# The key stage of a two-layer kernel rebuilt: tiles in pairs, places broadcast by DMA, four columns of entries summed at once, the weight table spread by two engines

## The chip, the cores and the metric

The kernel is one program on 1 core of a Trainium2 chip. The metric is device time in microseconds (us) for one execution. The kernel before takes 923.84 us in the median of 3 runs (919.55, 923.84, 924.43).

## The reference, cut to what matters

Two transformer-like layers run one after the other on x, which has 8 batches of 256 tokens of 512 numbers. Each layer is a "cond" part, then a feed-forward part, and is added to x. Only the first layer's preparation matters here.

- Cond part of layer 0: attention with a paged cache of keys and values. q, k and v are products of x; q and k are normalised and rotated; the new k and v are written into the cache; each query sees at most 256 keys that end at itself.
- Feed-forward part of layer 0: a gate picks 2 of 8 experts. Each expert's weight matrix is a common 512x512 matrix W plus a sparse correction. There are 4096 sparse entries with places `mask_idx` (row times 512 plus column) that all experts share. Places may repeat, and entries with the same place add up:

```python
deltas = softmax(expert_atom_weights, axis=-1) @ atoms        # (8, 64) @ (64, 4096)
weighted = deltas * sigmoid(importance)                       # (8, 4096)
rows = mask_idx // H
cols = mask_idx % H
vals = einsum('tk,tks->ts', rw, weighted[top_idx])
contrib = segment_sum((xt[:, cols] * vals).T, rows, num_segments=H)
out = xt @ W.T + contrib.T
```

## The kernel before, in words

Everything is float32. The engines are TensorE (PE; its weight loads are shown as PEld), VectorE (DVE), ScalarE (ACT), GpSimd (POOL) and SyncE (SP). SP only starts DMAs; ACT and POOL start some too. Each engine takes its instructions strictly in order. The order on each engine comes from a planner that replays the program with estimated times, except where the code pins it: `tc.keep_in_program_order`, `in_a_row` (L118: several products pinned behind each other), and the whole attention loop, whose PE order is written by hand (L1806).

The kernel's first stage, the stage of keys (L851 to L1578), makes everything that attention needs:

- **Keys and values.** `keys_values(i)` (L1367), for 16 tiles of 128 tokens: four 128x512 products into a PSUM bank `pkv` (three banks), an ACT copy into `kvt` (four buffers), the rotation on DVE (`rotated`, L1284), squares on ACT and their sum on DVE, a square root on ACT, four ACT multiplications, and one 256 KB store to `kv_new` in HBM.
- **The weight table.** `delta_d` in HBM holds, for each of the 512x512 places, 8 numbers, one for each expert (8 MB). It starts as W repeated 8 times: `load_base` (L1395) loads a 128x128 piece of W; `spread_base` (L1400) makes a 128x1024 tile `spread` of it with one ACT copy and stores it (512 KB). There are 16 such pieces and two `spread` buffers. Pieces are loaded in rounds 0 to 7 of the tile loop and spread in rounds 1 to 8.
- **The sparse entries.** 64 small products `pw` (L1438) turn the atoms into values in columns of 128 entries, 32 columns in all. `sum_same(k)` (L1490) treats one column: a PE transpose `prow` puts the 128 places of the column into every row, a DVE comparison gives `same` (which entries share a place), a DVE operation with `below` marks the entries that stood there before (`again`), a product `psm` sums the entries of a place for 8 experts, and ACT copies the result into `sums`. Three columns are done in each round from round 3. `find_places` (L1515) then sends every repeat to a spare row, so that each place is added once. Much later, during attention, POOL adds the sums into `delta_d` (`add_delta`, L1342).
- **Where the old keys lie.** DVE and POOL find blocks of the cache: four masks `near` (L1123 to L1131) are POOL's only long arithmetic in this stage; four small gathers `held_i` (L1099) read the block table. `find_rows(b)` (L1216) makes row lists; `gather_old(b)` (L1252) and `gather_new(b)` (L1261) are four POOL-issued gathers each, from the cache and from `kv_new`.
- **The end.** The queries of batches 0 and 1 are made, the gate's weights are folded through the output weights (`seen_through`, L130), `gather_new(0)` reads `kv_new`, and the loop of attention begins: the first score product is L1656, which needs `KT` (L1630), the turned keys of batch 0. DVE prepares the masks of attention from `posb` (L1634), whose memory was memory of the key stage.

SP's loads and stores stand in one queue in order: a store that waits for its tile holds back all that stand behind it. Each tile buffer that is stored can be written again only when its store has landed.

Of the kernel before, what the change touches and what calls it, by code (L numbers as in the profile page):

```python
# [19 lines left out]
P = 128  # L20
# [71 lines left out]
def two_layer_kernel(ctx: ExitStack, tc: tile.TileContext, io: dict, out: bass.AP):  # L92
# [759 lines left out]
    with ExitStack() as att:  # L852
# [28 lines left out]
        nc.scalar.dma_start(eaw[:, 0, :], io["eaw"])  # L881
        nc.sync.dma_start(blocks[0], xsrc[:, :, :512])

# [3 lines left out]
        nc.sync.dma_start(inv, io["inv_freq"].partition_broadcast(P))  # L887
        gains = {}
        for src in ("k_scale", "q_scale"):
            gains[src] = dp.tile([P, HD], F32, name=f"gain_{src}")  # L890
            nc.sync.dma_start(gains[src], io[src].partition_broadcast(P))
        for k in range(KC):
            nc.scalar.dma_start(wkv[:, k, :], wsrc[:, k, 512:])
        nc.sync.dma_start(blocks[1], xsrc[:, :, 512:1024])
        imp = dp.tile([P, NSC, E], F32, name="imp")
        nc.scalar.dma_start(
            imp.rearrange("p (q k) e -> p q (k e)", q=4),
            io["impT"].rearrange("(q p k) e -> p q (k e)", q=4, p=P),
        )
        mcol_i = dp.tile([P, NSC], I32, name="mcol_i")  # L900
        nc.scalar.dma_start(
            mcol_i.rearrange("p (q k) -> p q k", q=4),
            io["mask_idx"].rearrange("(q p k) -> p q k", q=4, p=P),
        )

        atoms = []
        for j in range(2):
            atoms.append(dp.tile([P, P, NSQ], F32, name=f"atoms{j}", tag="spread", bufs=2))
            for h in range(2):
                q = 2 * h + j  # L910
                nc.sync.dma_start(
                    atoms[j][h * ATOMS : (h + 1) * ATOMS],
                    io["atoms"][:, q * NS // 4 : (q + 1) * NS // 4].rearrange(
                        "a (p k) -> a p k", p=P
                    ),
                )
        for j in range(2, NTB + 1):
            cols = slice(j % NTB * 512, (j % NTB + 1) * 512)
            nc.sync.dma_start(blocks[j], xsrc[:, :, cols])
# [8 lines left out]
        nc.vector.reciprocal(esm, esm)  # L928
        nc.vector.tensor_scalar(share, share, esm, None, ALU.mult)
        nc.vector.tensor_copy(eaw[:, 1, :], share)  # L930

# [7 lines left out]
        for src in ("k_scale", "q_scale"):  # L939
            nc.vector.tensor_scalar(gains[src], gains[src], 1.0, None, ALU.add)  # L940
# [22 lines left out]
        for c in (C1, C2, C3):  # L963
            nc.vector.scalar_tensor_tensor(
                ang, turn, -c, ang, ALU.mult, ALU.add
            )

# [13 lines left out]
        nc.vector.tensor_scalar(nsin, sin, -1.0, None, ALU.mult)  # L981

        def with_gains(ctab, stab, src):
            g1 = gains[src][:, None, lo_].to_broadcast(trig)
            g2 = gains[src][:, None, hi_].to_broadcast(trig)
            nc.vector.tensor_tensor(ctab[:, :, lo_], cos, g1, ALU.mult)
            nc.vector.tensor_tensor(ctab[:, :, hi_], cos, g2, ALU.mult)
            nc.vector.tensor_tensor(stab[:, :, lo_], nsin, g2, ALU.mult)
            nc.vector.tensor_tensor(stab[:, :, hi_], sin, g1, ALU.mult)
# [143 lines left out]
        def find_blocks(psum, rs):  # L1133
# [51 lines left out]
        jf = ap.tile([P, B, NCAND], F32, name="jf")  # L1185
        nc.vector.tensor_copy(jf, j_i)
        nc.vector.tensor_tensor(
            jf, jf, slot0[:, :, None].to_broadcast([P, B, NCAND]), ALU.add
        )
        tbase = ap.tile([P, B, NCAND], F32, name="tbase")  # L1190
        nc.vector.scalar_tensor_tensor(
            tbase,
            jf,
            float(BLOCK),
            kvf[:, :, None].to_broadcast([P, B, NCAND]),
            ALU.mult,
            ALU.subtract,
        )
        nc.vector.tensor_scalar(
            jf, jf, float(NBLK - 1), SKIP, ALU.is_gt, ALU.mult  # L1200
        )
        nc.vector.tensor_tensor(tbase, tbase, jf, ALU.add)
# [5 lines left out]
        nc.vector.tensor_copy(code0, code_i)  # L1208
        nc.vector.tensor_tensor(code0, code0, tbase, ALU.add)
# [6 lines left out]
        def find_rows(b):  # L1216
# [5 lines left out]
            if b > 2:  # L1222
                tc.keep_in_program_order(first)
# [52 lines left out]
        def squares(src, heads, pool):  # L1276

            sq = pool.tile([P, heads, HD], F32, name="sq")
# [5 lines left out]
        def rotated(i, heads, src, ctab, stab, dst, pool):  # L1284
# [3 lines left out]
            xb = pool.tile(full, F32, name="xrot")  # L1288
# [12 lines left out]
        def query_parts(i, xcols, psum, tag, pool, early=False):  # L1301
# [10 lines left out]
            rotated(i, H, q3, qcos, qsin, qr, pool)  # L1312
            ms = squares(q3, H, pool)
# [47 lines left out]
        with proj:  # L1361
            qp = proj.enter_context(tc.tile_pool(name="qp", bufs=3))
            psq = proj.enter_context(tc.tile_pool(name="psq", bufs=3, space=PSUM))
            dw = proj.enter_context(tc.tile_pool(name="dw", bufs=3))
            psd = proj.enter_context(tc.tile_pool(name="psd", bufs=3, space=PSUM))

            def keys_values(i):  # L1367
# [3 lines left out]
                for k in range(KC):  # L1371
                    nc.tensor.matmul(  # L1372
# [6 lines left out]
                kvt = qp.tile([P, 2 * G * HD], F32, name="kvt", bufs=4)  # L1379
                nc.scalar.copy(kvt, pkv)  # L1380
                k3 = kvt[:, : G * HD].rearrange("p (h d) -> p h d", d=HD)
                kr = qp.tile([P, G, HD], F32, name="kr")
                rotated(i, G, k3, kcos, ksin, kr, qp)
                rs = squares(k3, G, qp)
                nc.scalar.activation(rs, rs, AF.Sqrt, bias=epss[:, 0:1], scale=1.0 / HD)
                nc.vector.reciprocal(rs, rs)
                for h in range(G):
                    nc.scalar.mul(k3[:, h, :], kr[:, h, :], rs[:, h : h + 1])
                nc.scalar.dma_start(kv_new[i * P : (i + 1) * P, :], kvt)
                return rs  # L1390

            QD = D // 4
            w0s = {}

            def load_base(c, part):  # L1395
                cols = slice(part * QD, (part + 1) * QD)
                w0s[c, part] = dw.tile([P, QD], F32, name="w0", bufs=4)
                nc.sync.dma_start(w0s[c, part], io["w0T"][c * P : (c + 1) * P, cols])

            def spread_base(c, part):  # L1400

                cols = slice(part * QD, (part + 1) * QD)
                w0 = w0s.pop((c, part))
                spread = dp.tile([P, QD, E], F32, name="spread", bufs=2)
                nc.scalar.copy(spread, w0[:, :, None].to_broadcast([P, QD, E]))
                wdst = delta_d[: D * D, :].rearrange("(c p r) e -> c p r e", p=P, r=D)
                nc.sync.dma_start(wdst[c][:, cols, :], spread)

            def base_weights(i):
                if i < 2 * KC:  # L1410
                    for part in (0, 1):
                        load_base(i // 2, i % 2 * 2 + part)
                if 1 <= i < 1 + 2 * KC:
                    for part in (0, 1):
                        spread_base((i - 1) // 2, (i - 1) % 2 * 2 + part)

            LEAD = 3
            for i in range(LEAD):
                keys_values(i)
                base_weights(i)  # L1420
                if i == 0:
                    pe = psd.tile([P, E], F32, name="pe", tag="psd")
                    nc.tensor.transpose(pe, eaw.rearrange("e h a -> e (h a)"), ident[:E, :E])
                    eawT = dp.tile([P, E], F32, name="eawT")
                    nc.scalar.copy(eawT, pe)
# [4 lines left out]
            pw = [  # L1430
                psd.tile([P, 2, NSQ, E], F32, name=f"pw{h}", tag=f"pw{h}", bufs=1)
                for h in range(2)
            ]
            for j in range(2):
                for k in range(NSQ):
                    for h in range(2):
                        rows = slice(h * ATOMS, (h + 1) * ATOMS)
                        nc.tensor.matmul(  # L1438
                            pw[h][:, j, k, :],
                            atoms[j][rows, :, k],  # L1440
                            eawT[rows, :],
                            start=True,
                            stop=True,
                        )
            nc.scalar.activation(imp, imp, AF.Sigmoid)
            weighted = dp.tile([P, NSC, E], F32, name="weighted")
            for h in range(2):
                span = slice(h * NSC // 2, (h + 1) * NSC // 2)
                nc.vector.tensor_tensor(
                    weighted[:, span, :],  # L1450
                    pw[h].rearrange("p j k e -> p (j k) e"),
                    imp[:, span, :],
                    ALU.mult,
                )


# [28 lines left out]
                pattern=[[-1, P]],  # L1485
                channel_multiplier=1,
# [3 lines left out]
            def sum_same(k):  # L1490
                prow = psd.tile([P, P], F32, name="prow", tag="psd")
                nc.tensor.transpose(
                    prow, mcol[:, k : k + 1].to_broadcast([P, P]), ident
                )
                same = dw.tile([P, P], F32, name="same")
                nc.vector.tensor_scalar(
                    same, prow, mcol[:, k : k + 1], None, ALU.is_equal
                )

                before = dw.tile([P, P], F32, name="before")  # L1500
                nc.vector.tensor_tensor_reduce(
                    out=before,
                    in0=same,
                    in1=below,
                    scale=1.0,
                    scalar=0.0,
                    op0=ALU.mult,
                    op1=ALU.max,
                    accum_out=again[:, k : k + 1],
                )  # L1510
                psm = psd.tile([P, E], F32, name="psm", tag="psd")
                nc.tensor.matmul(psm, same, weighted[:, k, :], start=True, stop=True)
# [993 lines left out]
```

## Time and profile before

| what | us |
|---|---|
| median of 3 runs (lowest, highest) | 923.84 (919.55, 924.43) |
| the profiled execution, own time | 923.56 |
| its span in the profile | 921.8 |
| so around the span | 1.8 |
| first key product starts | 8.28 |
| last of the four masks `near` ends | 43.68 |
| last store to `kv_new` issued | 100.61 |
| first gather from `kv_new` issued | 105.42 |
| first score product (end of the stage) | 117.57 |
| busy in 0 to 117.6: DVE, ACT, POOL | 87.3, 68.3, 45.3 |
| mean granted TensorE clock over the span | 0.989 |

How to read it: all times below count from the start of the span, and a time of the span plus 1.8 us is a time of the execution. The stage of keys is the first 117.6 us. From there to the end the program of the two versions is the same. "Landing" is the time from the start of a DMA's issue to its completion, when whoever waits for it may go on.

### The profile page before, as it was taken

To read this page: it belongs to the slowest core of one execution; us is meant where nothing else is said; L and a number is where in the kernel's file an instruction comes from. 1 tells how busy PE (TensorE), PEld (TensorE's weight loads), DVE (VectorE), ACT (ScalarE), POOL (GpSimd) and SP (SyncE) were. 2 spreads that over 40 slices of the span, in tenths; PEclk is the share of its full clock that TensorE was granted. 3 is DMA by queue.
4 is the path that set the end of the run, shared out by engine and by line. 5 is a ranking of instruction groups with operands and counts; after the bars stand their busy time and mean duration, and the time that the engine had idled before them with its cause. 6 is when DMAs were issued, how large, how long until landed. Compare 5 with 4: busy or idle time off the path is not lost. (4 is left out here: it accounts for less than half of the span.)

```text
span 921.8 us, 14079 instructions
## 1 busy us (share of the span) xinstructions
PE 877.9 (95%) x4740; PEld 478.5 (52%) x4740; DVE 469.4 (51%) x1510; ACT 362.2 (39%) x1005; POOL 368.1 (40%) x354
## 2 busy tenths in 40 slices
PE   6998989999999899989999999999999999999995
PEld 2654445555555455545443334546677776334773
DVE  4887879779778767684111112482022222455321
ACT  3676666665665556542222213411211111444110
POOL 3811355666667200062856752000333333344422
PEclk9899999999999999999999999999999999999998
DMA  7588494414522223084799966992544443333332
GB/s 204 197 315 295 142 300 135 127 23 107 149 69 57 78 77 99 19 293 103 170 290 340 208 112 160 394 333 109 186 101 72 72 75 69 58 59 58 71 39 42
DMA packets 73870, 133.82 MB, mean 145 GB/s; under 512 B 17262, under 2 KB 22894, under 8 KB 73665
## 3 DMA queue, kind: packets, MB, share of 16 engines
q0 software_dynamic: 25008, 43.42, 24.5%
q1 hardware_dynamic: 38208, 74.05, 23.0%
q10 hardware_dynamic: 10576, 15.39, 4.7%
q8 instruction: 40, 0.66, 0.3%
q14 instruction: 38, 0.30, 0.1%
HBM read 89.69 MB, written 51.78 MB: 153 GB/s over the span
## 5 line engine op out<-in xcount | busy, mean ns | idle before, releaser
L2381 DVE TENSOR_TENSOR y<-py,b 32x512 f32<-32x512 f32 (+1 forms) x60 | 41.3, 689 | 168.4 <-PE py L721 122.3
L2365 ACT ACTIVATE hs<-pu,b 128x32 f32<-128x32 f32 (+1 forms) x240 | 54.1, 349 | 169.9 <-PE pu L2339 138.9
L1688 ACT ACTIVATE s<-s,mx,roots 128x384 f32<-128x384 f32 x128 | 89.8, 703 | 53.1 <-DVE mx L1686 52.1
L707 POOL DMA_INDIRECT xs<-g_d,from_i_l x33 | 34.2, 1037 | 173.8 <-issue 87.9
L750 DVE COPY xsT<-pa 128x512 f32<-128x512 f32 x59 | 40.5, 687 | 101.5 <-PE pa L744 101.2
L2339 PE MATMUL pu<-xsT,w 128*128 128x128 f32 x768 | 89.8, 275 | 0.4 <-issue 0.4
L2339 PEld LDWEIGHTS pu<-xsT,w 128*128 128x128 f32 x768 | 87.7, 192 | 1.1 <-ACT g L2252 0.6
L721 PE MATMUL py<-w,hs 128*128 128x512 f32 x192 | 86.3, 593 | 0.0
L1372 PE MATMUL pkv<-wkv,xb 128*128 128x512 f32 x128 | 67.2, 651 | 8.3 <-DMA wkv<-wqkvT 8.3
L767 POOL DMA_INDIRECT out<-y,token_i_l x33 | 50.9, 1544 | 58.0 <-DVE y L2383 31.2
L1673 DVE CUSTOM_DVE_ANT_0 s<-ps,mask 128x384 f32<-128x384 f32 x128 | 67.4, 549 | 6.3 <-PE ps L1656 6.3
L1344 POOL DMA_INDIRECT delta_d<-entries,put_i x32 | 50.9, 1590 | 45.5 <-DMA delta_d<-entries,put_i 36.2
L731 PE MATMUL py<-delta,xsT 128*64 128x512 f32 (+1 forms) x288 | 65.5, 598 | 0.0
L1723 PE MATMUL po<-pT,kv 128*64 128x256 f32 x384 | 57.4, 388 | 7.9 <-ACT pT L1713 4.9
L1711 PEld LDWEIGHTS pp<-ident,s 128*128 128x128 f32 x384 | 42.1, 141 | 37.0 <-issue 23.9
L1305 PE MATMUL pq<-wq,xb 128*128 128x512 f32 x128 | 60.3, 595 | 0.7 <-DVE lg L1753 0.7
L836 PE MATMUL ph<-woT,oT 128*128 128x512 f32 x128 | 60.8, 609 | 0.0
L721 PE MATMUL py<-delta,xsT 128*128 128x512 f32 x128 | 58.5, 596 | 0.0
L2244 PE MATMUL pc<-wc,x1T 128*128 128x512 f32 x128 | 58.5, 596 | 0.0
L1711 PE MATMUL pp<-ident,s 128*128 128x128 f32 x384 | 56.3, 280 | 2.3 <-DVE pT L1713 1.3
L767 POOL DMA_INDIRECT sums_d<-y,token_i_l x26 | 41.2, 1583 | 32.6 <-DMA sums_d<-y,token_i_l 11.8
L1656 PE MATMUL ps<-KT,QT 64*128 64x384 f32 x256 | 53.7, 520 | 0.4 <-DVE KT L1630 0.4
(436 smaller groups left out, 1467.8 us busy)
## 6 DMA issues: line engine op xcount, KB each, us to landing
delta_d<-spread SPq DMA_DIRECT2D x16, 512.0 KB, 5.4
raw<-delta_d SPq DMA_DIRECT2D x16, 512.0 KB, 4.4
w<-fc_w SPq DMA_DIRECT2D x8, 1024.0 KB, 16.2
part<-sums_d SPq DMA_DIRECT2D x32, 256.0 KB, 4.9
w<-fc_w SPq DMA_DIRECT2D x8, 768.0 KB, 10.6
xb<-xT SPq DMA_DIRECT2D x5, 1024.0 KB, 6.0
sums_d<-zero SPq DMA_DIRECT2D x18, 256.0 KB, 5.7
kv_new<-kvt ACTq DMA_DIRECT2D x16, 256.0 KB, 3.5
```

The source lines that it names most:

```text
L721: nc.tensor.matmul(py, xT[:, k, :], of_expert(experts[0])(weights(k)), start=(k == 0), stop=(k == KC - 1),)
L731: lambda k=k, h=h: nc.tensor.matmul(py[h * n : (h + 1) * n, :], xT[:, k, h * n : (h + 1) * n], of_expert(experts[h])(weights(k)), start=(k ...
L767: nc.gpsimd.indirect_dma_start(out=sum_d, out_offset=bass.IndirectOffsetOnAxis(ap=token, axis=0), in_=y, in_offset=None, bounds_check=sum_ ...
L836: nc.tensor.matmul(ph, oTs[i // 2][:, k, (i % 2) * P : (i % 2 + 1) * P], woT[:, k, :], start=(k == 0), stop=(k == KC - 1),)
L1305: nc.tensor.matmul(pq, xcols[:, k, :], wq[:, k, :], start=(k == 0), stop=(k == KC - 1))
L1372: nc.tensor.matmul(pkv, xb[:, k, cols], wkv[:, k, :], start=(k == 0), stop=(k == KC - 1),)
L1673: nc.vector.tensor_tensor_reduce(out=s, in0=ps[:, r, :WU], in1=mask[:, t, :], scale=1.0, scalar=NEG, op0=ALU.add, op1=ALU.max, accum_out=m ...
L1688: nc.scalar.activation(ss[r], ss[r], AF.Exp, bias=mx[:, r : r + 1], scale=root[:, r : r + 1], accum_out=sm[:, r : r + 1],)
L1711: nc.tensor.transpose(pp[:, c, :], part, ident)
L1723: nc.tensor.matmul(po[r * HD : (r + 1) * HD].rearrange("p m q -> p (m q)"), kvs[t + c][:, v0 + r * HD : v0 + (r + 1) * HD], pT[:, 3 * r + ...
L2244: nc.tensor.matmul(pc, x1T[:, k, i * P : (i + 1) * P], wc[:, k, :], start=False, stop=(k == KC - 1),)
L2339: nc.tensor.matmul(pu[:, c, :], w1[:, k, plan.full[s], c * P : (c + 1) * P], xsT[:, k, :], start=(k == 0), stop=(k == KC - 1),)
```

## The change

- **Order of the first loads.** The key weights go first on ACT's queue; the first block of x is loaded in two parts, 128 columns ahead; the second block waits for the first weights. The gains are loaded on ACT's queue and used later; `imp` and `mcol_i` move to SP behind the atoms.
- **Keys in pairs.** Two tiles share one `kvt` (two buffers of a pair); rotation, squares, sum, root and reciprocal are done once for a pair with twice the width; one 512 KB store for a pair. The eight multiplications of a pair remain.
- **The weight table.** The 16 pieces are split in halves of 128x512. The first half of each is spread by POOL (a multiplication by 1.0) into `spread0`, which has one buffer, the second by ACT into `spread1`, which has two; each half is stored by itself (256 KB, 2 KB to a partition), 32 stores in all. Loads are in rounds 5 to 12, spreading in rounds 6 to 13.
- **Values of the entries.** Instead of 64 products with 8 columns each, four products 32x512, one for each group of 32 PSUM partitions, an ACT copy, four transposes and eight DVE products.
- **Sums.** Four columns at a time, in rounds 8 to 15. The places are broadcast to all partitions by four 512 KB DMAs (`spread_places`) and copied by ACT into `prow`; DVE makes `same` and `first` 512 wide; eight products (32x128 and 8x128) go to four groups of partitions of one bank; ACT copies, PE transposes once, ACT copies and DVE takes a minimum.
- **Placement.** `LEAD` is 5 instead of 3 (the entries start after five tiles), `find_candidates` and the query gains move to rounds 6 and 7, several operations are pinned in program order.

```diff
-        nc.scalar.dma_start(eaw[:, 0, :], io["eaw"])
-        nc.sync.dma_start(blocks[0], xsrc[:, :, :512])
+        for k in range(KC):
+            nc.scalar.dma_start(wkv[:, k, :], wsrc[:, k, 512:])
+        nc.sync.dma_start(blocks[0][:, :, :P], xsrc[:, :, :P])
+        nc.sync.dma_start(eaw[:, 0, :], io["eaw"])
...
+        nc.sync.dma_start(blocks[0][:, :, P:], xsrc[:, :, P:512])
...
+        nc.vector.tensor_copy(blocks[1][:, 0, :1], wkv[:, 0, :1])
         nc.sync.dma_start(blocks[1], xsrc[:, :, 512:1024])
...
-                kvt = qp.tile([P, 2 * G * HD], F32, name="kvt", bufs=4)
-                nc.scalar.copy(kvt, pkv)
...
+                t = i % 2
+                if t == 0:
+                    pair.append(qp.tile([P, 2, 2 * G * HD], F32, name="kvt"))
+                kvt = pair[-1]
+                nc.scalar.copy(kvt[:, t, :], pkv)
+                if t == 0:
+                    return None
...
-                nc.scalar.dma_start(kv_new[i * P : (i + 1) * P, :], kvt)
...
+                nc.scalar.dma_start(
+                    kv_new[(i - 1) * P : (i + 1) * P, :].rearrange("(t p) c -> p t c", p=P), kvt
+                )
...
-            QD = D // 4
+            QD = D // 8
...
             def spread_base(c, part):
...
-                spread = dp.tile([P, QD, E], F32, name="spread", bufs=2)
-                nc.scalar.copy(spread, w0[:, :, None].to_broadcast([P, QD, E]))
...
-                nc.sync.dma_start(wdst[c][:, cols, :], spread)
...
+                for h in range(2):
+                    cols = slice((2 * part + h) * QD, (2 * part + h + 1) * QD)
+                    spread = dp.tile([P, QD, E], F32, name=f"spread{h}", bufs=1 + h)
+                    of_all = w0[:, h * QD : (h + 1) * QD, None].to_broadcast([P, QD, E])
+                    if h:
+                        nc.scalar.copy(spread, of_all)
+                    else:
+                        nc.gpsimd.tensor_scalar(spread, of_all, 1.0, None, ALU.mult)
+                    nc.sync.dma_start(wdst[c][:, cols, :], spread)
...
-            LEAD = 3
+            LEAD = 5
...
+            pw = psd.tile([P, 512], F32, name="pw", tag="pw0", bufs=1)
+            in_a_row(
+                (
+                lambda g=g: nc.tensor.matmul(
+                    pw[g * BW : (g + 1) * BW, :].rearrange("c (k p) -> c k p", p=P),
+                    eawT,
+                    atoms[g // 2][:, :, g % 2 * NG : (g % 2 + 1) * NG].rearrange("r p k -> r k p"),
...
-                prow = psd.tile([P, P], F32, name="prow", tag="psd")
-                nc.tensor.transpose(
-                    prow, mcol[:, k : k + 1].to_broadcast([P, P]), ident
-                )
...
+            def spread_places(q):
...
+                nc.sync.dma_start(
+                    rows_i[q], io["mask_idx"][q * n : (q + 1) * n].partition_broadcast(P)
+                )
...
+            def sum_same(k0):
+                ks = slice(k0, k0 + SAME)
+                each = [P, SAME, P]
+                prow = dw.tile(each, F32, name="prow", bufs=2)
...
+                nc.vector.tensor_tensor(
+                    same, prow, mcol[:, ks, None].to_broadcast(each), ALU.is_equal
+                )
...
+                nc.vector.tensor_tensor(
+                    first, same, below[:, None, :].to_broadcast(each), ALU.mult
+                )
+                psm = psd.tile([P, P], F32, name="psm", tag="psd")
...
+                        psm[j * BW : (j + 1) * BW, :],
+                        unit,
+                        first[:, j, :],
...
+                        psm[j * BW : j * BW + E, :],
+                        weighted[:, k0 + j, :],
+                        same[:, j, :],
...
+                nc.tensor.transpose(pst.rearrange("p j c -> p (j c)"), wide, ident)
+                nc.scalar.copy(sums[:, ks, :], pst[:, :, :E])
+                nc.vector.tensor_scalar(again[:, ks], pst[:, :, E], 1.0, None, ALU.min)
...
-                base_weights(i)
...
+                parts = [(c, part) for c in range(KC) for part in range(4)]
+                n0 = 2 * (i - LEAD)
+                for at in parts[n0 : n0 + 2]:
+                    load_base(*at)
+                if i > LEAD:
+                    for at in parts[n0 - 2 : n0]:
+                        spread_base(*at)
...
-                for k in range(summed, min(summed + 3, NSC)):
-                    sum_same(k)
-                    summed = k + 1
+                if i >= 8 and summed < NSC:
+                    sum_same(summed)
+                    summed += SAME
```

## The prediction

> **What bounds the kernel now.** I read, in this order: the page's busy shares, the stretches of the first stage, its groups of instructions, then the timeline of POOL, DVE and PE. The page's chain of waits covers only the last store, so the stage is read from stretches. They show core busy times of PE, PEld, DVE, ACT, POOL, then the clock, the DMA share and GB/s:
>
> ```profile
> 0.00:20.00 20.00, 11.72 (x22) 5.04 (x23) 8.22 (x42) 5.74 (x9) 6.93 (x46) 1.00 0.79 228
> 20.00:30.00 10.00, 10.00 (x69) 8.56 (x68) 9.31 (x38) 5.11 (x8) 7.29 (x6) 0.85 0.23 69
> 30.00:80.00 50.00, 50.00 (x178) 26.31 (x177) 41.04 (x179) 35.60 (x110) 21.18 (x23) 0.96 0.84 296
> 80.00:105.00 25.00, 22.51 (x78) 12.02 (x77) 19.90 (x81) 16.82 (x57) 0.00 (x0) 0.93 0.47 175
> ```
>
> PE has work nearly all the time, DVE 82% of it from 30 to 80; POOL is light. So before, PE with DVE sets the pace of the stage. Its end is in the timeline: gathers of new keys (POOL), the masks' first step (DVE), the first score (PE).
>
> ```profile
> 105.42 1.00 POOL L1267 DMA_INDIRECT kv<-kv_new,idx_new  x1 [29.08 <-DMA kv_new<-kvt]
> 108.04 0.48 DVE L1634 TENSOR_SCALAR posb<-keyf,kvf 128x512 f32<-128x512 f32 x1
> 117.58 0.59 PE L1656 MATMUL ps<-KT,QT 64*128 64x384 f32 x2 [0.42 <-DVE KT L1630]
> ```
>
> From there attention keeps PE busy 176.8 of 182.4 us to 300, so a shift of the first score passes whole to the end. I predict that shift.
>
> **What gets cheaper** (rows of the stage):
>
> ```profile
> L1405 ACT COPY spread<-w 128x1024 f32<-128x1024 f32 x16 | 16.5, 1040 | 6.8 <-DMA delta_d<-spread 3.5 <-PE pw L1438 3.1 <-ACT sums L1513 0.2
> L1496 DVE TENSOR_SCALAR same<-prow,mcol 128x128 f32<-128x128 f32 x32 | 11.2, 349 | 10.4 <-PE prow L1492 9.6
> L1438 PE MATMUL pw<-eawT,atoms 64*128 64x8 f32 x64 | 7.8, 380 | 0.0
> ```
>
> - DVE, sums: removed 32 x (0.349 same + 0.288 before + 0.081 read) = 23.0. Added 8 x (two 512-wide operations at 0.68, the row of the 512-wide sum L1299, + 0.16) = 12.2. DVE, keys: 16 tiles cost 9.1 + 6.8 + 6.6 + 6.6 + 2.7 = 31.8; 8 pairs cost 8 x (2 x 0.41 + 2 x 0.68 + 0.67 + 0.17) = 24.2. Net -18.4.
> - ACT: removed 16.5 (spread) + 6.5 (squares) + 4.8 (roots) + 4.5 (sums) = 32.3; added 16 x 0.59 + 8 x 0.59 + 8 x 0.30 + 8 x (0.59 + 0.28 + 0.2) + 0.6 = 25.7. Net -6.6. The multiplications and the copies of `pkv` stay.
> - PE: `pw` 7.8 becomes 1.5 to 3.1 (L140, four 512-wide records in 1.53) + 0.6 for transposes. The slow clock behind it goes too: 0.85 and 0.81 in 20 to 40 are 3.4 us lost. A column costs 1.14 - 0.86 = 0.28 between two key records, 9.0 in all; eight groups of eight products and a transpose cost 0.6 each if four groups of partitions overlap, 2.0 if not: 4.8 to 16. Net -14 to 0.
> - Start: the first product waited until 8.28 for 256 KB of weights behind 1 MB of x; with 256 KB of x ahead I estimate 5, bounds 3 and 8.3.
> - DMA: +2 MB of broadcast places, 7 us at 296 GB/s, spread over the stage.
>
> By these sums the stage could lose 10 to 14 us. That is a rival, because of the next part.
>
> **What is added on POOL.** In the compiled order POOL does the four `near` masks, the block gathers, then 16 spreads, with the old-cache gathers between them; the first gather from `kv_new` comes after the 15th spread, its other three after the 16th. `spread0` has one buffer, and the instructions wait so: every POOL spread waits until the store of the one before has landed. That is a serial chain of 16 x (compute + hand-over + landing). The end hangs on it twice: on the gathers, and on `posb`, whose memory was the spreads': it waits for the last landing, and DVE's queue of masks, fold and `KT` waits behind it.
>
> ```profile
> L1126 POOL TENSOR_SCALAR near<-far,offp 128x256 f32<-128x256 f32 x4 | 4.4, 1094 | 14.2 <-DVE look L1086 14.1
> L1130 POOL TENSOR_SCALAR near<-near 128x256 f32<-128x256 f32 x4 | 3.7, 920 | 0.2
> L815 POOL COPY delta<-raw 128x1024 f32<-128x1024 f32 x4 | 8.2, 2040 | 5.0 <-DMA raw<-delta_d 5.0
> ```
>
> - *Compute C.* No POOL multiplication of 512 is in the trace. Above: twice L1130, 1.84. Below: half of L815's copy of 1024, 1.02. The row is nearer to the same kind of instruction, with some fixed share: 1.55.
> - *Landing L* of a 256 KB store with 2 KB to a partition is that of `kv_new`; of a 512 KB spread, the second line:
>
> ```profile
> DMA to landing us min/median/max: 2.0/3.5/8.6
> DMA to landing us min/median/max: 2.6/5.4/8.1
> ```
>
>   Bounds 2.0 (quiet) and 8.6. The stage carries 2 MB more than before but stretches; I take 3.2, just under the median. SP's start of the store follows its tile within 0.05 (25.62 + 1.04 to 26.69).
> - *Period* P = 1.55 + 0.05 + 3.2 = 4.8, bounds 3.1 and 10.5.
> - *Start of the chain.* `near` begins when DVE has `far`: 21.6 before. Now DVE must first sum the squares of the first pair: product from 5, first tile 6.2 (as 8.28 to 14.45), second 3.6, copy and squares 1.2, sum 0.7, `far` 0.5: 17.2. `near` and block gathers took 21.71 to 43.68, 22.0. So 39.2; bounds 36 and 43.7.
> - *Gathers inside:* eight at 1.3 (start to start); three in a row take 3.9 against a landing of 3.2, twice: +1.4; row lists that come late: +0.6. Together 2, bounds 0 and 8.
> - *Tail:* from `posb` to the first score 117.57 - 108.04 = 9.5.
>
> Sum: 39.2 + 16 x 4.8 + 2 + 9.5 = 127.5, against 117.57: +9.9. On the profiled execution's own 923.56 that is **933.5**; the median of the runs, 923.84, stands 0.3 above it. The savings of DVE, ACT and PE then lie beside the chain and are worth nothing. ACT's spreads have two buffers, but their stores stand between POOL's in SP's queue, so ACT too is paced by it, and PE behind ACT's `pkv` copies.
>
> Costed at nothing: the moved gains and `imp` (needed later than they land), `find_candidates`, the pins, all covered by the chain; without that cover they are inside the 104 of rival 1. Moving the first weight loads of W from the first rounds behind LEAD costs nothing to the chain, since POOL is not free before 39 anyway.
>
> [...] I stay at the trace's 3.2, since the queues of this stage are not quiet.
>
> [...]
>
> **The rivals.**
> 1. *The stores land quietly and the chain is short* (faster). With C 1.3 and L 2.2 the period is 3.55 and the score would come at 107.5; the other end is PE: 88 of products (55 keys, 13.8 queries, the rest 19) + 5 start + 3 cold clock + about 8 of waits = 104. First score at 104 to 111, so 910 to 917, say **913**. For it: median landings of `kv_new` of 2.0 to 2.3 in 80 to 105. Against it: in 30 to 80 the DMA engines are 84% busy. It decides below a period of 4.2, where 39.2 + 16 P + 11.5 = 117.57.
> 2. [...] Two blocks of x, `wq` and `woT` stand right ahead of POOL's stores on SP; spreads landed in 7.4 to 8.1 in 50 to 60 and 70 to 80. With C 1.8 and L 3.9 the period is 5.75: 39.2 + 92 + 4 + 9.5 = 144.7, **951**.
> 3. *It doesn't matter*: a period of 3.9 to 4.5, within 0.5%, about **924**: the gain of three engines is eaten by the fourth.
>
> **The numbers.** Forecast (periods 4.5 to 5.4) 0.42, rival 2 0.18, rival 3 0.16, rival 1 0.24. Differences within 0.5% (919.2 to 928.5) can't be told from none in this kernel. Faster 0.24, same 0.16, slower 0.60. The range reaches from within rival 1 to rival 2: 911 to 951; forecast and rival 2 alone span 928.5 to 951.
>
> **What would show it.** In the profile after: POOL's spreads with idle time before them released by the DMA `delta_d<-spread`, one period of 4.8 from start to start, the last near 113; DVE, ACT and PE with more idle time than before although their busy sums fall by about 18, 7 and up to 14; `posb` released by that landing; first score near 127. Right in mechanism and wrong in size if only the period differs. Wrong altogether if the spreads follow each other without waiting for a store, if `near` ends before 34, or if the first score waits for PE or for `kv_new` and not for POOL. A half clock after a long PE idle time at the start of attention would add up to 3 us that I have not counted.

## The result and the profile after

| | before | after |
|---|---|---|
| median of 4 runs (lowest, highest), us | 923.60 (919.55, 924.43) | 937.13 (933.57, 941.24) |
| ratio, 95% interval | 1 | 1.0145 [1.0111, 1.0179] |
| the profiled execution: own time, span | 923.56, 921.8 | 941.24, 939.4 |
| first key product starts | 8.28 | 5.08 |
| last `near` ends, first POOL spread starts | 43.68, none | 40.6, 40.60 |
| `posb` starts | 108.04 | 122.88 |
| first score product | 117.57 | 135.29 |

The changed kernel is slower by 13.5 us (forecast: 9.9). The profiled execution of after is the slowest of its four runs, so its own times are read against its span: the first score is 17.7 us later than before, and the span 17.6 us longer. The shift passes whole to the end. The median of before is of one run more than in the table ahead of the prediction. The ratios and intervals, here and below, are those of the record; they differ from the quotients of the medians by up to 0.35% (e5 below: 0.9996, quotient 1.0030), so no smaller difference is read.

The stretches of after; columns as in the table of before (busy PE, PEld, DVE, ACT, POOL, then the clock, the DMA share and GB/s):

```profile
0.00:20.00 20.00, 13.29 (x24) 5.19 (x24) 10.16 (x49) 5.48 (x9) 7.91 (x50) 1.00 0.84 228
20.00:30.00 10.00, 10.00 (x28) 3.73 (x28) 9.93 (x25) 7.25 (x19) 9.67 (x11) 1.00 0.37 123
30.00:80.00 50.00, 41.53 (x147) 19.87 (x145) 29.03 (x85) 27.10 (x71) 29.34 (x23) 0.86 0.71 237
80.00:105.00 25.00, 17.22 (x80) 7.28 (x79) 13.39 (x41) 14.97 (x42) 10.16 (x7) 0.86 0.73 252
```

Between 30 and 105, PE falls from 72.5 us of work to 58.8, DVE from 60.9 to 42.4, ACT from 52.4 to 42.1, and the clock is lower too. Part of the fall is work that is gone (for DVE 16.3 us over the whole stage, as worked out below); the rest is idle time of three engines in a longer stage. POOL's timeline in after says what the stage waits for (start, duration, and in brackets the idle time ahead with what ended it):

```profile
19.17 2.06 POOL L1135 TENSOR_SCALAR near<-far,offp 128x256 f32<-128x256 f32 x2 [11.43 <-DVE far L1129]
...
40.60 1.53 POOL L1453 TENSOR_SCALAR spread<-w 128x512 f32<-128x512 f32 x1
...
50.20 1.66 POOL L1453 TENSOR_SCALAR spread<-w 128x512 f32<-128x512 f32 x1 [4.38 <-DMA delta_d<-spread]
55.02 1.49 POOL L1453 TENSOR_SCALAR spread<-w 128x512 f32<-128x512 f32 x1 [3.17 <-DMA delta_d<-spread]
...
94.13 1.49 POOL L1453 TENSOR_SCALAR spread<-w 128x512 f32<-128x512 f32 x1 [5.90 <-DMA delta_d<-spread]
97.79 1.49 POOL L1453 TENSOR_SCALAR spread<-w 128x512 f32<-128x512 f32 x1 [2.17 <-DMA delta_d<-spread]
102.95 1.49 POOL L1453 TENSOR_SCALAR spread<-w 128x512 f32<-128x512 f32 x1 [3.68 <-DMA delta_d<-spread]
106.70 1.59 POOL L1453 TENSOR_SCALAR spread<-w 128x512 f32<-128x512 f32 x1 [2.26 <-DMA delta_d<-spread]
...
116.92 1.09 POOL L1279 DMA_INDIRECT kv<-kv_new,idx_new  x1 [0.16 <-issue]
118.92 1.49 POOL L1453 TENSOR_SCALAR spread<-w 128x512 f32<-128x512 f32 x1 [0.92 <-issue]
```

This is the chain of the prediction. The profile names the landing of a store ahead of eight of the fifteen spreads that follow the first; ahead of five more it says only "issue", but there too a store landed 0.14 to 0.15 us before the spread began (63.50 ahead of 63.64, for one). The other two, at 69.69 and 81.12, stand right behind gathers. The sixteen take from 40.60 to 120.4, one each 5.22 us ((118.92 - 40.60) / 15). The first gather from `kv_new` stands behind the fifteenth. DVE's timeline shows the other hook:

```profile
122.88 0.49 DVE L1730 TENSOR_SCALAR posb<-keyf,kvf 128x512 f32<-128x512 f32 x1 [3.29 <-DMA delta_d<-spread]
```

`posb` waits for the last landing, as predicted, 14.8 us later than before. Behind it DVE holds back ACT's `wn`, and ACT holds back PE (PE's timeline):

```profile
120.83 1.04 PE L140 MATMUL acc<-wn,gw 128*32 128x512 f32 x2 [2.43 <-ACT wn L139]
...
125.46 3.64 PE L140 MATMUL acc<-wn,gw 128*32 128x512 f32 x6 [3.00 <-ACT wn L139]
...
135.29 1.01 PE L1752 MATMUL ps<-KT,QT 64*128 64x384 f32 x2
```

### The profile page after: what moved, and what is told of

It reads as the page before. It is cut to its first block, busy times and chain, and to the rows that moved or that the text cites. A ratio compares the mean times of both kernels' runs of the same rounds, so it can differ in the third digit from the quotient of the medians.

```text
span 939.4 us, 13996 instructions
## 1 busy us (share of the span) xinstructions
PE 879.9 (94%) x4728; PEld 469.5 (50%) x4728; DVE 465.1 (50%) x1397; ACT 361.6 (38%) x984; POOL 397.5 (42%) x373
## 5 line engine op out<-in xcount | busy, mean ns | idle before, releaser
L1387 PE MATMUL pkv<-wkv,xb 128*128 128x512 f32 x128 | 63.4, 643 | 6.7 <-DMA xb<-xT 5.1
L1317 PE MATMUL pq<-wq,xb 128*128 128x512 f32 x128 | 62.4, 614 | 0.7 <-DVE lg L1849 0.7
```

The costliest lines, as they stand in the source:

```text
L1317: nc.tensor.matmul(pq, xcols[:, k, :], wq[:, k, :], start=(k == 0), stop=(k == KC - 1))
L1387: product = nc.tensor.matmul(pkv, xb[:, k, cols], wkv[:, k, :], start=(k == 0), stop=(k == KC - 1),)
```

## The experiments

**Theory:** POOL's part of the spreading sets the end, through its chain of compute and landing in one buffer. **Rivals:** the DMA queues are full whoever makes the tiles; POOL's late start at 40.6 counts and not its buffer; other parts of the change lose the time.

The kernels ran in four groups, each on one chip with runs of the kernel before, whose median there was 924.55 (first four), 923.46 (next four), 920.98 (next three) and 923.62 (last). So kernels of different groups are compared by ratio. A first score is that of one profiled execution, which need not be the median one (e5's took 928.82 us, its median is 926.19).

| kernel | median | ratio [95%] | first score | from `posb` to it |
|---|---|---|---|---|
| before | 923.60 | 1 | 117.57 | 9.5 |
| after | 937.13 | 1.0145 [1.0111, 1.0179] | 135.29 | 12.4 |
| e1 no wait for the store | (988.18) | not comparable | 114.83 | 10.1 |
| e2 three buffers in turn | 932.14 | 1.0107 [1.0041, 1.0173] | 127.22 | 17.2 |
| e3 all on ACT | 933.09 | 1.0092 [1.0056, 1.0128] | 129.92 | 16.1 |
| e4 two buffers for POOL | 929.88 | 1.0057 [1.0027, 1.0087] | 125.67 | 10.3 |
| e5 spread as before | 926.19 | 0.9996 [0.9967, 1.0025] | 123.70 | 12.3 |
| e6 the same, early | 925.65 | 1.0017 [0.9984, 1.0050] | 124.13 | 11.6 |
| e7 two buffers, ACT first | 926.16 | 1.0020 [0.9987, 1.0052] | 124.04 | 13.7 |
| e8 POOL's own queue | 954.78 | 1.0320 [1.0265, 1.0374] | 151.85 | 11.9 |
| e9 as e5, no pairs | 920.84 | 1.0016 [0.9991, 1.0040] | 117.03 | 10.1 |
| e10 as e5, no sums of four | 929.23 | 1.0095 [1.0057, 1.0132] | 130.20 | 17.1 |
| e11 DVE in POOL's place | 919.92 | 0.9989 [0.9965, 1.0013] | 115.72 | 10.1 |
| e12 e11's and e9's edits | 922.12 | 0.9988 [0.9966, 1.0011] | 119.08 | 14.6 |

**e1: POOL waits for no landing.** ACT's tile is stored into both places, POOL's into none:

```diff
-                    nc.sync.dma_start(wdst[c][:, cols, :], spread)
+                    if h:
+                        nc.sync.dma_start(wdst[c][:, cols, :], spread)
+                        other = slice(2 * part * QD, (2 * part + 1) * QD)
+                        nc.sync.dma_start(wdst[c][:, other, :], spread)
```

> POOL still makes its half of each spread, but what is stored in its place is ACT's half a second time (so half of the base weights are wrong): same bytes, same number of stores, POOL waits for no landing. Theory (chain of compute and landing on POOL with one buffer): POOL's spreads follow at 1.5 to 2 us wherever their weights are there, the last ends before 105, the first score comes at 104 to 113 instead of 135.3, the time is 908 to 917. Rival A (the 8 MB of stores and 2 MB of places load the DMA queues, whoever makes the tiles): the first score stays above 128, the time above 930. Rival B (tail: new gathers, POOL's late start): first score 118 to 128, 920 to 930.

With these other numbers in the table the later stages take longer: from the first score to the end of the span it is 869.8 us here, and 800 to 805 in all other kernels. Why was not looked into; only its first stage is read. POOL's timeline, then PE's:

```profile
40.20 9.54 POOL L1453 TENSOR_SCALAR spread<-w 128x512 f32<-128x512 f32 x6
...
89.74 3.60 POOL L1453 TENSOR_SCALAR spread<-w 128x512 f32<-128x512 f32 x2 [3.21 <-DMA w<-w0T]
```

```profile
114.83 1.56 PE L1755 MATMUL ps<-KT,QT 64*128 64x384 f32 x8 [0.46 <-issue]
```

Six spreads follow each other at 1.59 us, the last ends at 93.3, and the first score is 20.5 us earlier than in after, with the same number of bytes and stores. Full queues, rival A, are refuted. The edit takes away two waits at once, POOL's for landings and SP's for POOL's tiles (59.5 us in after), so it shows that the cost is POOL's part in the stores, not how the two waits share it. The first score lies 1.8 us above my 104 to 113, which comes up again below.

**e2, e3 and e4: other buffers, other engine.** e2 lets both engines take three buffers in turn:

```diff
-                    spread = dp.tile([P, QD, E], F32, name=f"spread{h}", bufs=1 + h)
+                    spread = dp.tile([P, QD, E], F32, name="spread", bufs=3)
```

e3 has this too, and makes all 32 tiles on ACT:

```diff
-                    if h:
-                        nc.scalar.copy(spread, of_all)
-                    else:
-                        nc.gpsimd.tensor_scalar(spread, of_all, 1.0, None, ALU.mult)
+                    nc.scalar.copy(spread, of_all)
```

e4 gives POOL two buffers:

```diff
-                    spread = dp.tile([P, QD, E], F32, name=f"spread{h}", bufs=1 + h)
+                    spread = dp.tile([P, QD, E], F32, name=f"spread{h}", bufs=2)
-                prow = dw.tile(each, F32, name="prow", bufs=2)
+                prow = dw.tile(each, F32, name="prow", bufs=1)
```

> The same three buffers, but both engines take them in turn instead of one for POOL and two for ACT. A tile is free three spreads later, so a chain of three POOL spreads holds two landings and not three. Theory: period 2.9 to 3.5 instead of 5.2, the first score at 108 to 120, the time 911 to 923. Rival A (queues full): unchanged, above 930. Rival B (late start of POOL, to which ACT is now tied as well): first score above 120, 923 to 930.

> ACT makes all 32 spreads, with three buffers in turn; POOL none. Nothing then waits for near's end at 40.6. Theory: ACT has 71.0 + 9.9 = 81 us busy of the stage, PE becomes the bound: first score 104 to 112, time 907 to 916. Rival A (queues full): above 930. Rival C (ACT waits for landings in POOL's stead, and PE behind ACT's copies): first score 115 to 130, 918 to 933.

> POOL has two buffers as ACT has; to make room prow has one buffer instead of two. Theory: period (1.5 + 3.3)/2 = 2.4 to 2.6, so POOL has all spread by about 90 and the chain is no bound; the late start at 40.6, behind which ACT's second pair of spreads waits (10.1 us in the trace), stays: first score 106 to 118, time 910 to 921. Rival A: above 930.

All three missed: 932.1, 933.1 and 929.9, where the theory wanted 907 to 923 (e3 ended at the far edge of its rival C). The times of e2 and e3 even lie above 930, which I had put down as the sign of rival A; e1 and, below, e11 speak against that rival, with the same stores. The direction held (a second buffer took back 0.9% by the ratios, some 8 us, and the last spread ended at 101 instead of 120), the size didn't. Three things stayed. The first is the late start of POOL. ACT's and PE's timelines of e4:

```profile
43.21 0.59 ACT L1400 COPY kvt<-pkv 128x512 f32<-128x512 f32 x1 [10.98 <-DMA delta_d<-spread]
```

```profile
43.85 5.32 PE L1387 MATMUL pkv<-wkv,xb 128*128 128x512 f32 x6 [5.30 <-ACT kvt L1400]
```

The copy of a key tile is put down to a store's landing, 10.98 us; the profile names the last releaser it sees, and which instruction behind it counted isn't certain here. In after the chain is plainer: ACT's third spread sits idle 10.07 us until 44.94, since its first two tiles' stores stand in SP's queue behind POOL's first, which is made at 40.6. The second is SP's queue. With two buffers POOL still waits for landings in e4, 18.9 us in all, most of it here:

```profile
63.08 1.49 POOL L1453 TENSOR_SCALAR spread<-w 128x512 f32<-128x512 f32 x1 [12.05 <-DMA delta_d<-spread]
```

The stores were ready (POOL's sixth spread ends at 51.03), but the load of `wq` stands ahead of them in SP's queue, and the write of ACT that it waits for came only at 55.33 and took 0.17. The third is the clock. Stretches of e2, then of e4, with the clock third from the end:

```profile
117.60:131.00 13.40, 11.33 (x35) 5.99 (x34) 5.53 (x17) 3.13 (x5) 8.81 (x9) 0.54 0.81 263
```

```profile
117.60:131.00 13.40, 10.86 (x49) 5.40 (x50) 9.57 (x27) 5.71 (x11) 9.53 (x10) 1.00 0.95 301
```

e2 and e3 go through their last 13 us at about half the clock (0.54 in both) and take 17.2 and 16.1 from `posb` to the score, e4 10.3.

**e5, e6 and e7: the start.** e5 and e6 put back the 512 KB tiles that ACT alone makes in two buffers, in the new rounds and in the old ones. e7 is e4 with ACT making POOL's first four spreads.

```diff
-                for h in range(2):
-                    cols = slice((2 * part + h) * QD, (2 * part + h + 1) * QD)
-                    spread = dp.tile([P, QD, E], F32, name=f"spread{h}", bufs=1 + h)
...
+                cols = slice(2 * part * QD, 2 * (part + 1) * QD)
+                spread = dp.tile([P, 2 * QD, E], F32, name="spread", bufs=2)
+                nc.scalar.copy(spread, w0[:, :, None].to_broadcast([P, 2 * QD, E]))
+                nc.sync.dma_start(wdst[c][:, cols, :], spread)
```

```diff
-                    if h:
+                    if h or c == 0:
                         nc.scalar.copy(spread, of_all)
```

> The rest of the change stays, but the table is spread as before: ACT alone, 16 tiles of 512 KB, two buffers (prow has one buffer for room), loads and spreads still in rounds 5 to 13. After the first four runs: taking the chain's waits away gave back only 4 to 7 of 13.5 us, and its first score came at 114.8 even without any wait. Theory (the rest is the start: ACT's second pair of spreads, and PE behind it, wait until SP has sent POOL's first spread at 42): no POOL spread, so first score at 108 to 117, time 913 to 923. Rival D (the other parts of the change lose it: pairs of key tiles, 512-wide sums, spreads five rounds later): first score 121 to 130, time 926 to 936, as in the run with all spreads on ACT.

> As the kernel before in this call, with loads of the table in rounds 0 to 7 and spreads in 1 to 8 instead of 5 to 12 and 6 to 13. If the place behind LEAD is free of cost, as I put it, equal to the run beside it within 2 us. If lateness of the table costs (stores collide with wq, woT and the places, and posb waits for the last), 4 to 10 us faster than it: first score 104 to 112, time 908 to 918.

> POOL has two buffers, and the first four of its sixteen spreads are made by ACT instead, so that SP's queue doesn't wait for the end of near. Theory (start): PE's idle time between 30 and 60 falls from 10 to under 4, ACT's wait for landings from 17 (two buffers for POOL) to under 8; first score 5 to 10 earlier than the 125.7 of two buffers alone: 115 to 121, time 919 to 925. Rival (start costs nothing): 925 to 931.

e5 takes only the two-engine spreading out, and the kernel is as fast as before, 0.9996 [0.9967, 1.0025]. So, within that interval, all of the loss is in that part, and the rest of the change together is worth nothing measurable. But my theory wanted more, a gain, and missed: both the time, 926.19, and the first score fell where I had put rival D (121 to 130, 926 to 936). PE's timeline of e5:

```profile
123.70 1.56 PE L1747 MATMUL ps<-KT,QT 64*128 64x384 f32 x8 [0.42 <-DVE KT L1721]
```

Part of that late score is a slow start of this execution: `near` begins at 22.0, in e6 at 22.5 and in e7 at 21.1, against 17.9 in e4. The granted clock of the first 20 us belongs to it: 0.83 in e5 and e6, 0.91 in e7, 1.00 in e4. e6 is equal to e5 within 0.6 us: moving the loads and spreads behind LEAD cost nothing measurable, as I had put it. e7, in the same group, reaches 1.0020 with POOL still making twelve of the tiles, against 1.0057 of e4, but the intervals overlap, and its 926.16 lies in the range of its rival, "start costs nothing" (925 to 931). What the late start is worth stays open. Its first score of 124.0 missed my 115 to 121 by 3.0, and its `near` began 3.2 later than in e4.

**e8: POOL's stores from POOL's own queue.** One line, buffers as in after:

```diff
-                    nc.sync.dma_start(wdst[c][:, cols, :], spread)
+                    (nc.sync if h else nc.gpsimd).dma_start(wdst[c][:, cols, :], spread)
```

> One change from the changed kernel: POOL's stores are issued by POOL itself and not by SP, so ACT's stores and the loads behind them don't wait for POOL. The chain on POOL stays (one buffer). Theory, both halves: ACT's wait for landings falls from 21.9 to under 8 and PE's 8.2 near 42 goes, but the last spread still ends at 110 to 121 and posb waits for it: first score 124 to 134, time 927 to 937. If SP's queue were the whole cause: first score under 118, time under 922. If POOL's own issue costs more than it saves: period over 5.5, time over 940.

The third case came: 954.8. The views of one tile (durations min/median/max, first and last start) show that POOL's instruction is no longer than in after, but now POOL issues, too:

```profile
L1453 POOL TENSOR_SCALAR spread<-w x16: 1479/1490/1732, 40.4 to 135.4; 128x512 f32<-128x512 f32 x16
L1454 POOL DMA_DIRECT2D delta_d<-spread x16: 586/597/646, 42.2 to 137.2; - x16
```

The last spread and the first score (POOL's and PE's timelines):

```profile
135.41 1.49 POOL L1453 TENSOR_SCALAR spread<-w 128x512 f32<-128x512 f32 x1 [2.32 <-DMA delta_d<-spread]
```

```profile
151.85 1.56 PE L1752 MATMUL ps<-KT,QT 64*128 64x384 f32 x8 [1.37 <-issue]
```

The period is (135.41 - 40.40) / 15 = 6.33 and not 5.22. 15 x 1.11 = 16.7 us are to be expected at the first score, and it is 16.6 later (151.85). By the ratios the time is 1.75% more, some 16 us. That is the theory's best witness: the chain became longer, and the end stays 16.4 us behind the start of the last spread in both kernels (135.29 - 118.92, 151.85 - 135.41). POOL's issue explains 0.9 of the 1.11 (0.60 for itself and 0.30 ahead of it); SP's order changed with it, so the period is not all that moved. My second hope failed. ACT's wait for landings didn't fall below 8 but rose to 40.2, because SP still waits for POOL, now with the loads of W:

```profile
66.96 9.05 SPq L1440 DMA_DIRECT2D w<-w0T  x2
...
82.66 7.30 SPq L1440 DMA_DIRECT2D w<-w0T  x2
```

A load needs a free `w0`, which POOL's spread frees, and ACT's stores stand behind the load.

**e9 and e10: what the rest is worth.** Both are e5 with one more part undone: e9 handles key tiles one at a time as before; e10 compares column by column, with PE's transposes and without the 2 MB of places.

```diff
-                if t == 0:
-                    pair.append(qp.tile([P, 2, 2 * G * HD], F32, name="kvt"))
-                kvt = pair[-1]
...
+                kvt = qp.tile([P, 2 * G * HD], F32, name="kvt", bufs=4)
+                nc.scalar.copy(kvt, pkv)
...
+                rotated(i, G, k3, kcos, ksin, kr, qp, 2)
```

```diff
-                same = dw.tile(each, F32, name="same", bufs=1)
...
+                for k in range(k0, k0 + SAME):
+                    prow = psd.tile([P, P], F32, name="prow", tag="psd")
+                    nc.tensor.transpose(
+                        prow, mcol[:, k : k + 1].to_broadcast([P, P]), ident
+                    )
```

> Table spread as before (as in e5_before_spread, first score 123.7, 926.2 in the median), and the pairs of key tiles undone too: one tile at a time, kr, xrot and sq of 256 with two or three buffers. Tells what pairing gives or takes once POOL's chain is gone. If pairs cost (near waits for the second tile's squares, ACT waited 6.4 for the store of a pair): first score 115 to 120, time 917 to 922. If pairs gain as I summed (DVE 7.6, ACT 4): 928 to 934. If neither: within 2 us of 926.

> Table spread as before (as in e5_before_spread), pairs kept, and the entries compared one column at a time as before, their places again turned by PE, no broadcast of places (2 MB less). If the four columns side by side gain what I summed for DVE and PE (DVE 10.8, PE up to 9): 930 to 936. If the casts of the broadcast places (1.12 each on ACT, I had put 0.59) and the 2 MB take it back: within 2 us of 926. If they cost more than they give: under 922.

Without pairs 1.0016: the pairs give nothing measurable (e5 0.9996; the intervals overlap), although `near` starts at 16.4 without them. Its bare numbers, 117.03 and 920.84, lie where I had put "pairs cost", but before ran at 920.98 in this group. Without the sums of four 1.0095: in this arrangement they are worth some 9 us, part of which is the clock again (0.59 and 0.55 in 105 to 131). Since e5 as a whole equals before, something else in the arrangement costs about as much; which part (the sums start in round 8 and no longer in round 3, the start, the order of the loads) no run separates.

**e11: DVE in POOL's place.** Sixteen stores of 256 KB for each engine as in after, three buffers in turn as in e2; only the engine differs from e2:

```diff
-                        nc.gpsimd.tensor_scalar(spread, of_all, 1.0, None, ALU.mult)
+                        nc.vector.tensor_copy(spread, of_all)
```

> DVE takes POOL's half of the spreads, three buffers in turn between DVE and ACT; all else as in the changed kernel. Theory (POOL's late start and its single buffer were the loss, DVE is free early): DVE's copy is 0.35 to 0.7, 6 to 11 us of its spare time; first score 114 to 122, time 916 to 924, 13 to 21 below the changed kernel. Rival (waiting for landings now holds DVE's queue, and PE's and ACT's behind it): 928 to 936, as with all on ACT.

919.92, ratio 0.9989 [0.9965, 1.0013]; e2 with POOL has 1.0107 [1.0041, 1.0173]. The view of the tile, and PE's timeline:

```profile
L1453 DVE COPY spread<-w x16: 375/427/578, 27.4 to 98.5; 128x512 f32<-128x512 f32 x16
```

```profile
82.83 1.12 PE L1317 MATMUL pq<-wq,xb 128*128 128x512 f32 x2
...
106.95 1.05 PE L140 MATMUL acc<-wn,gw 128*32 128x512 f32 x2 [3.17 <-ACT wn L139]
...
115.72 0.59 PE L1752 MATMUL ps<-KT,QT 64*128 64x384 f32 x2 [0.42 <-DVE KT L1726]
```

DVE begins at 27.4, while POOL is at its masks until 40.6, and takes 0.43 us where POOL takes 1.50.

**e12: the two cheapest edits together,** with e9's `keys_values`:

```diff
-                    spread = dp.tile([P, QD, E], F32, name=f"spread{h}", bufs=1 + h)
+                    spread = dp.tile([P, QD, E], F32, name=f"spread{h}", bufs=2)
...
-                        nc.gpsimd.tensor_scalar(spread, of_all, 1.0, None, ALU.mult)
+                        nc.vector.tensor_copy(spread, of_all)
...
-                prow = dw.tile(each, F32, name="prow", bufs=2)
+                prow = dw.tile(each, F32, name="prow", bufs=1)
```

> The two cheapest edits together: DVE makes POOL's half of the spreads (two buffers each for DVE and ACT, prow one), and key tiles go one at a time. If their gains add (near may start at 16.4 instead of 17.7 to 22, and no chain on POOL): 0.4 to 1.0% under the kernel before of this call, first score 110 to 114. If the stage's end is now set by the chain of the last keys and queries on ACT, DVE and PE, which neither edit shortens: within 0.3% of before, first score 115 to 118. If DVE, which gets back the small key operations, becomes late: over 0.3% slower.

0.9988 [0.9966, 1.0011]: within 0.3% of before, the second case; its first score, 119.08, lies 1.1 above what that case named. The gains don't add, and no version of this study beats the kernel before measurably.

## Why the prediction was right, and where its sizes were off

- **The bound that takes over: right.** POOL's spreads wait for landings, `posb` waits for the last, and the shift passes whole to the end. e1 takes the waits away (first score -20.5), e8 lengthens the period (+16.6 for 15 x 1.11), e5 and e11 take POOL out (ratio 1.00). How the loss divides between the one buffer, the late start, SP's order and the clock is argued from e2, e4 and e7, not shown.
- **Start 39.2: measured 40.6.** The first product came at 5.08, as put. But I let the first tile run on, and it stopped at 10.54 for 1.63 us until another piece of the weights came; `near` began at 19.2 and not 17.2. `near` and the block gathers took 21.4 (22.0 put).
- **Compute 1.55: measured 1.50.** Taking the row of the like instruction, with less than twice its time, was right.
- **Period 4.8 and 2 for the gathers: measured 5.22 with them** (put: 4.93). This is the largest term of the error in the chain, 4.3 us from the first start to the last; from there to `posb` it is 3.96, so 1.0 less than put. A quiet period is 3.7 (102.95 to 106.70), so a landing and hand-over of 2.2; the middle, from 44 to 94, with 1 MB loads, places and loads of W in the same queue and eight gathers on POOL, has 4.0 to 8.6, 6.2 in the mean. At 3.7 throughout, rival 1's condition (below 4.2) would have held; its "quiet stores" were true of six of the fifteen periods only (3.65 to 3.97).
- **Tail 9.5: measured 12.4.** I counted `posb` as one wait. DVE holds the queries' last sums behind it, ACT its `wn`, and PE then waits 5.4 us for `wn`, partly at a lower clock (0.84 and 0.70 from 117.6 to 141). This is the half clock that I named and didn't count, "up to 3": the clock stood at 0.50 from 126.70 to 136.94, behind 3.00 us of idle PE.
- **The sum:** 127.5 put, 135.3 in the profiled execution: 1.4 from the start, 3.5 from the first spread to `posb`, 2.9 from the tail. All three were put too low, so nothing cancelled. That execution is the slowest of four; the median lies 3.6 above the forecast.
- **"The savings lie beside the chain and are worth nothing": right as to the result, wrong as to why.** With the chain gone they are worth nothing either (e5, e11). The term ACT -6.6 was wrong. Its rows of after:

```profile
L1451 ACT COPY spread<-w 128x512 f32<-128x512 f32 x16 | 9.8, 617 | 22.5 <-DMA delta_d<-spread 21.9 <-DMA w<-w0T 0.6
...
L1554 ACT CAST prow<-rows_i 128x512 f32<-128x512 int32 x8 | 9.0, 1121 | 0.0
```

  The cast of the places takes 1.12 where I put 0.59, and a second loading of the root's table adds 1.28; with them 32.3 removed stand against 31.7 added. For DVE I find 38.5 added (25.8 for keys, 12.7 for sums) against 54.8 removed: -16.3, put -18.4. The four groups of partitions do overlap: eight 128-wide products took 0.43 us (106.15), eight 128-wide transposes over all partitions 1.04 (114.33).
- **Rival 1's end of 104 was wrong.** With no chain the first score comes at 114.8 (e1) and 115.7 (e11). PE does reach the queries at 82.8 in e11, before at 90.5; but from there to the score it takes 32.9 and not 27.1, with groups of sums between and 3.2 us of waiting for ACT's `wn`. I had summed PE's work and eight us of waits. My reading is that I left out that the stage ends in a chain of short steps over ACT, DVE and PE that no saved busy time shortens; no run shortens that chain to show it.
- **POOL beside DVE, and the landing.** The 1.8 that rival 2's sum takes for a spread on POOL is shown by no run: in after the sixteen took 1.486, 1.496 and 1.847 us as lowest, median and highest. DVE was slower beside a spread at times: `first` at 110.58 took 1.09 and not 0.69, `late` at 115.42 took 0.48 and not 0.16; most others kept their time. From the end of a spread to the start of the next, the landing between them, it took 2.2 us in the quiet period and up to 7.1, from a store issued at 56.54 to the spread at 63.64, and that decided.

## What to carry to other kernels

A tile that is stored costs its buffer for compute and landing (here 1.50 us, and 2.2 to 7.1 from its end to the next start); with one buffer, the engine's free time was no capacity (POOL's 24.8 us of spreads took 79.8), and the work moved to an idle engine became a chain of (compute + landing) x count, sixteen spreads 5.22 us apart, that started when that engine's other duties ended, at 40.6. Look first at where the chain starts, how many buffers it has, and what stands behind its stores in the issuing queue; the engine's busy share shows none of it. The same work went to DVE, 3.5 times as fast there (0.43 us against 1.50) and free 13 us sooner, without measurable loss. And the sums of saved busy time gave no gain in this stage, which ends in a chain of short steps: look for such a chain.

## What was not expected of the hardware

- How much goes with the granted clock of PE at the end of the stage: from `posb` to the first score it takes 9.5 to 12.3 us where the clock is 1.00 in the stretches from 105 to 131 (before, e1, e4, e5, e9, e11), and 16.1 to 17.2 where it falls to 0.54 or 0.55 (e2, e3, e10). No run changes the clock alone.
- When the clock falls. In the traces of before and after the granted clock stands at 0.50 in these stretches of the first 140 us: 26.97 to 33.80 and 85.00 to 88.41 (before), 44.78 to 58.43, 95.97 to 102.80 and 126.70 to 136.94 (after); they last 3.41 us or two, three or four times as long. Four of the five began in or soon after idle time of PE: behind 2.49 us in before; within 8.25 and 4.51 us, and behind 3.00, in after. The first of before began with PE in its row of 64 small products and no idle time, and the 8.28 idle us at the start of before left the clock at 1.00. Nor does the length of the idle time tell the cases apart: the first `acc` took 1.91 us behind idle times of 2.48 and 3.06 us (e6, e12; granted clock 0.86 and 0.73 in 105 to 117.6), and 1.04 and 1.05 behind 3.17 in e5 and e11 (clock 1.00). What decides it is not shown.
- ACT's cast of 512 int32 with a stride of eight elements took 1.12 us, its copies of 512 contiguous floats out of PSUM 0.58. Whether the stride or the type costs it was not tried.
- A DMA issued by POOL held POOL for 0.60 us (e8), and 0.30 passed ahead of it where it stood right behind its spread; the same store issued by SP took SP 0.34 (median, after).
